# Interleaving the later stages of an image pipeline with its matrix-root stage on one TensorE

## The chip, the cores and the metric

The kernel runs on one core of one Trainium2 chip. The metric is the device time of one execution in microseconds (us). The kernel before takes 3546 us, with runs within 0.1% of each other.

## The reference, cut to what matters

`x` is 32 images of 32 channels of 128x128, float32. Two layers follow each other:

```python
def _L0_conv_ref(A):             # per channel matrix: square root by 5 Newton-Schulz steps
    Y = A2 / normA; Z = I
    for _ in range(5):
        T = 0.5 * (3.0 * I - Z @ Y)
        Y = Y @ T
        Z = T @ Z
    return Y * sqrt(normA)

def _L1_conv_ref(x, w1, w2):     # spectral layer: keep 64 x 32 modes, mix channels, go back
    x_dht = fftn(x).real
    top = einsum('bixy,ioxy->boxy', x_dht[:, :, :32, :32], w1)
    bot = einsum('bixy,ioxy->boxy', x_dht[:, :, -32:, :32], w2)
    ...
    return ifftn(out_dht).real

x = x + _L0_conv_ref(group_norm(x))
x = x + _L1_conv_ref(group_norm(x), weights1, weights2)
```

In the kernel the first layer is a chain of 128x128 matrix products for each of 1024 channel matrices ("root steps"). The second is, per image, a forward transform, then for all images together the products with the weights ("mode products"), then per image an inverse transform that is added to the layer's input.

## The kernel before

There are three stages, one after the other. The root stage runs four lanes, each a set of four channels, with the forward transforms woven in. Each image stays in one 2 MB tile and goes to DRAM (`mid`) with one store.

```python
while todo or any(lanes) or back:
    for i in range(LANES):
        ...                               # start a set, or take one step of lane i (newton)
    rounds += 1
    if back and next(back[0], back) is back:      # one step of statistics or forward transform
        back.pop(0)
```

Then come the mode products over 16 groups kk of modes. The weights come in three buffers, and the spectra of four kk at a time in 2 MB:

```python
for kk in range(KK):
    wt = wts[kk % 3]
    for l4 in range(4):
        nc.sync.dma_start(out=wt[rows, l4], in_=wk[kk, rows])
    if kk % 4 == 0:
        nc.scalar.dma_start(out=xk, in_=xs[:, :, kk : kk + 4, :]...)
    for h in range(2):
        ...                               # 16 matmuls into one PSUM bank, then a copy to om
    for q in range(4):
        nc.sync.dma_start(out=od[:, :, KK * q + kk], in_=om[32 * q : 32 * q + 32]...)
```

Then the inverses, where loads stand on one DMA queue (sync) and stores on another (scalar):

```python
for b in range(B):
    nc.sync.dma_start(out=ob, in_=od[b]...)
    nc.sync.dma_start(out=xt, in_=mid[b])
    for d in range(2):
        ...     # 32 matmuls of 64x32 into two banks (pg), per e: copy to gt, 2 matmuls of 512 (py)
                nc.vector.tensor_add(xt[:, o : o + 4, :], py[i], xt[:, o : o + 4, :])
    for i in range(2):
        nc.scalar.dma_start(out=out[b, :, 16 * i : 16 * i + 16, :], in_=xt[...])
```

Of the kernel before, what the change touches and what calls it, by code (L numbers as in the profile page):

```python
# [31 lines left out]
LANES = 4  # L33

# [18 lines left out]
def conv_preact_kernel(  # L53
# [35 lines left out]
    xs = dram.tile([B, P, KK, 32], F32, name="xs")  # L89
    od = dram.tile([B, 2, K, 16, L], F32, name="od")  # L90

    with ExitStack() as phase:
        xp = phase.enter_context(tc.tile_pool(name="xp", bufs=3))
        up = phase.enter_context(tc.tile_pool(name="up", bufs=1))
        nsp = phase.enter_context(tc.tile_pool(name="nsp", bufs=5))
        sp = phase.enter_context(tc.tile_pool(name="sp", bufs=2))
        small = phase.enter_context(tc.tile_pool(name="small", bufs=2))
        ps_ns = phase.enter_context(tc.tile_pool(name="ps_ns", bufs=5, space=PSUM))
        ps_ax = phase.enter_context(tc.tile_pool(name="ps_ax", bufs=2, space=PSUM))
        ps_st = phase.enter_context(tc.tile_pool(name="ps_st", bufs=1, space=PSUM))  # L100

        def root(v, n, tag, f=1.0):

            s0 = small.tile([P, n], F32, tag=f"{tag}_s0", name=f"{tag}_s0")
            nc.scalar.activation(s0, v, AF.Sqrt, scale=1.0 / (f * f))
            q = small.tile([P, n], F32, tag=f"{tag}_q", name=f"{tag}_q")
            nc.vector.reciprocal(q, s0)
            nc.vector.tensor_mul(q, q, v)
            nc.vector.scalar_tensor_tensor(q, q, 1.0 / (f * f), s0, ALU.mult, ALU.add)
            s = small.tile([P, n], F32, tag=f"{tag}_s", name=f"{tag}_s")  # L110
            nc.vector.tensor_scalar_mul(s, q, 0.5 * f)
            return s

        def moments(st, tag):



            f = st.rearrange("p (g c) (e t) -> p g (c e) t", c=2, t=3)
            ms = small.tile([P, G], F32, tag=f"{tag}_ms", name=f"{tag}_ms")
            nc.vector.tensor_reduce(ms, f[:, :, :, 1], AX.X, ALU.add)  # L120
            pm = ps_st.tile([P, 64], F32, tag="st", name=f"{tag}_pm")
            nc.tensor.matmul(pm[:, 0:G], avg_mean, ms, start=True, stop=True)
            nm = small.tile([P, G], F32, tag=f"{tag}_nm", name=f"{tag}_nm")
            nc.vector.tensor_copy(nm, pm[:, 0:G])  # L124
            d = small.tile([P, G, 4], F32, tag=f"{tag}_d", name=f"{tag}_d")
            nc.vector.tensor_tensor(
                d, f[:, :, :, 1], nm[:, :, None].to_broadcast([P, G, 4]), ALU.add
            )
            nc.vector.tensor_mul(d, d, d)
            nc.vector.scalar_tensor_tensor(  # L130
                d, d, 64.0, f[:, :, :, 2], ALU.mult, ALU.add
            )
            return ms, nm, d

        def prep(b, made):

            xt = xp.tile([P, C, P], F32, tag="xt", name=f"xt{b}")
            for i in range(4):
                nc.sync.dma_start(
                    out=xt[:, 8 * i : 8 * i + 8, :],  # L140
                    in_=xt_in[b, :, 8 * i : 8 * i + 8, :],
                )
            yield
            st = small.tile([P, C, 6], F32, tag="a_st", name=f"a_st{b}")
            for c in range(C):
                nc.vector.bn_stats(st[:, c, :], xt[:, c, :])
                if c % 8 == 7:
                    yield
            _, nm, d = moments(st, "a")
            q = small.tile([P, C], F32, tag="a_qs", name=f"a_qs{b}")  # L150
            nc.vector.tensor_reduce(
                q, d.rearrange("p g (c e) -> p (g c) e", e=2), AX.X, ALU.add
            )
            pq = ps_st.tile([P, 64], F32, tag="st", name=f"a_pq{b}")
            nc.tensor.matmul(pq[:, 0:C], avg_q, q, start=True, stop=True)
            yield

            v = small.tile([P, C + G], F32, tag="a_v", name=f"a_v{b}")
            nc.vector.tensor_copy(v[:, 0:C], pq[:, 0:C])
            vg = small.tile([P, G], F32, tag="a_vg", name=f"a_vg{b}")  # L160
            nc.vector.tensor_reduce(
                vg, v[:, 0:C].rearrange("p (g c) -> p g c", c=2), AX.X, ALU.add
            )
            nc.vector.tensor_scalar(v[:, C:], vg, 0.5, EPS, ALU.mult, ALU.add)
            s = root(v, C + G, "a_r")
            inv = small.tile([P, C + G], F32, tag="a_inv", name=f"a_inv{b}")
            nc.vector.reciprocal(inv, s)
            yield

            sc = small.tile([P, C], F32, tag="a_sc", name=f"a_sc{b}")  # L170
            nc.vector.tensor_scalar_mul(sc, inv[:, 0:C], 1.0 / P)
            n = small.tile([P, G, 2], F32, tag="a_n", name=f"a_n{b}")
            nc.vector.tensor_tensor(
                n,
                s[:, 0:C].rearrange("p (g c) -> p g c", c=2),
                inv[:, C:, None].to_broadcast([P, G, 2]),
                ALU.mult,
            )
            nn = small.tile([P, C], F32, tag="a_nn", name=f"a_nn{b}")
            nc.vector.tensor_scalar_mul(nn, n.rearrange("p g c -> p (g c)"), float(P))  # L180
            sn = root(nn, C, "a_t")

            scr = small.tile([P, C], F32, tag="a_scr", name=f"a_scr{b}")
            nc.vector.tensor_scalar_mul(scr, sc, QR)
            off = small.tile([P, G, 2], F32, tag="a_off", name=f"a_off{b}")
            nc.vector.tensor_tensor(
                off,
                scr.rearrange("p (g c) -> p g c", c=2),
                nm[:, :, None].to_broadcast([P, G, 2]),
                ALU.mult,  # L190
            )
            made[b] = (xt, nm, sc, sn, scr, off.rearrange("p g c -> p (g c)"))
            yield

        def bank(pool, tag):
            return pool.tile([P, 4, P], F32, tag=tag, name=tag)

        def taken(ps, tag, bufs=5, f=1.0):
            t = nsp.tile([P, 4, P], F32, tag=tag, name=tag, bufs=bufs)
            if f == 1.0:  # L200
                nc.scalar.copy(t, ps)  # L201
            else:
                nc.scalar.mul(t, ps, f)  # L203
            return t

        def plus(ps, f, t, tag, bufs=5):

            s = nsp.tile([P, 4, P], F32, tag=tag, name=tag, bufs=bufs)
            nc.vector.scalar_tensor_tensor(s, ps, f, t, ALU.mult, ALU.add)  # L209
            return s  # L210

        def products(lhsT, rhs):
            ps = bank(ps_ns, "ns")
            for j in range(4):
                nc.tensor.matmul(  # L215
                    ps[:, j, :], lhsT[:, j, :], rhs[:, j, :], start=True, stop=True
                )
            return ps

        def transposed(t):  # L220
            ps = bank(ps_ns, "ns")
            for j in range(4):
                nc.tensor.transpose(ps[:, j, :], t[:, j, :], ident)  # L223
            return ps

        raw = {}

        def fetch(b, g):
            t = nsp.tile([P, 4, P], F32, tag="b", name=f"b{b}_{g}", bufs=7)
            nc.sync.dma_start(  # L230
                out=t, in_=x[b, 4 * g : 4 * g + 4].rearrange("c h w -> h c w")
            )
            raw[b, g] = t

        def quartic(m, mb, r):


            v = plus(products(mb, m), -1 / (QA * QR), m, "v", 4)
            yield
            w = plus(transposed(v), -QA, r, "w", 4)  # L240
            yield
            q = plus(products(v, w), -QA / 16, eyes["eye_q"], "q")
            yield
            return q

        def newton(b, g, xt, nm, sc, sn, scr, off):


            chans = range(4 * g, 4 * g + 4)
            m = nsp.tile([P, 4, P], F32, tag="x", name="x0", bufs=6)  # L250
            mb = raw.pop((b, g))
            for j, c in enumerate(chans):
                nc.gpsimd.tensor_scalar(  # L253
                    m[:, j, :],
                    xt[:, c, :],
                    nm[:, c // 2 : c // 2 + 1],
                    sc[:, c : c + 1],
                    ALU.add,
# [32 lines left out]
            yield  # L291

        def post(b, xt):

            nc.sync.dma_start(out=mid[b], in_=xt)


# [263 lines left out]
```

## Time and profile before

| stretch of the profiled run | us | TensorE busy us | granted clock | DMA share |
|---|---|---|---|---|
| root stage | 0 to 3043 | 2997 | 1.00 | 0.20 |
| last spectrum and mode products | 3043 to about 3190 | a third | 0.69 in the middle | 0.75 |
| inverses | about 3190 to 3543 | two thirds | 0.83 | 0.96 |

The table reads: TensorE is full for 86% of the time while the DMA engines are a fifth busy, and then the DMA engines are full or nearly so and TensorE is not. "Granted clock" is the TensorE clock that the profile shows as allowed, as a share of full speed. "PE" is TensorE executing matmuls and "PEld" its weight loads. "DVE", "ACT" and "POOL" are VectorE, ScalarE and GpSimd. "SPq" is the in-order queue from which the sync engine issues transfers. A line such as "A <- B" says that A sat idle until B was done.

### The profile page before, as it was taken

The numbers are of one execution on the slowest core, as the hardware profiler recorded it, in microseconds if no ns is written. First come the engines' busy times: TensorE is split into PE (matmuls) and PEld (weight loads), VectorE is DVE, ScalarE is ACT, GpSimd is POOL, SyncE is SP. The second block draws the span as 40 slices with busy tenths as digits, with TensorE's granted clock in tenths as the row PEclk, the third lists the DMA queues.
The fourth block names the chain that finished last, engine by engine and source line by source line (L and its number), as shares of the span: only waits on it lengthen the run. The fifth ranks groups of instructions, "written<-read, shape, count | busy, mean of one in ns | idle before, by whom it ended". The sixth has DMA issues, their size and how long they took to land.

```text
span 3543.4 us, 77025 instructions
## 1 busy us (share of the span) xinstructions
PE 3297.4 (93%) x30912; PEld 2962.0 (84%) x30912; DVE 2302.1 (65%) x6401; ACT 1422.0 (40%) x2993; POOL 1092.1 (31%) x1544
## 2 busy tenths in 40 slices
PE   6999999999999999999999999999999999536776
PEld 6999999999999999999999999999999999433433
DVE  6666777776677677776667777776777765203544
ACT  4444444444444444444444444444444443101211
POOL 4333333333333333333333333333333332100000
PEclk9999999999999999999999999999999999777888
DMA  3221122221222222222221122211222210569999
GB/s 114 72 75 68 57 72 75 75 72 52 73 75 73 75 73 72 72 75 72 75 72 55 69 75 75 73 58 67 75 72 75 72 52 31 144 163 403 418 416 386
DMA packets 206390, 382.74 MB, mean 108 GB/s; under 512 B 11345, under 2 KB 158801, under 8 KB 189649
## 3 DMA queue, kind: packets, MB, share of 16 engines
q1 hardware_dynamic: 180368, 302.33, 24.2%
q10 hardware_dynamic: 25664, 75.50, 5.5%
q8 instruction: 243, 3.98, 0.5%
q14 instruction: 115, 0.93, 0.1%
HBM read 226.79 MB, written 150.99 MB: 107 GB/s over the span
## 4 chain that ended last, share of the span: by engine, by line
PE 83%; DMA 9%; DVE 3%; issue 2%; ACT 1%; SPq 1%; POOL 1%; ACTq 0%; DVEq 0%; POOLq 0%
PE ns L215 62%; PE ns L223 9%; PE ax L302 5%; DMA out<-yt 3%; DMA yt<-mid 2%; PE py L503 2%; DMA b<-in_x 2%; PE f L327 2%; PE ax L314 2%; DMA xk<-xs 1%; ACT spec L370 1%; PE pm L443 1%; POOL x L253 1%; DVE xt L288 1%; SPq L457 1%
## 5 line engine op out<-in xcount | busy, mean ns | idle before, releaser
L278 POOL TENSOR_TENSOR r<-mb,eye_d 128x512 f32<-128x512 f32 x256 | 325.3, 1271 | 1397.7 <-ACT mb L203 1190.3
L253 POOL TENSOR_SCALAR x<-xt,a_nm,a_sc 128x128 f32<-128x128 f32 x1024 | 445.2, 449 | 542.8 <-PE ns L215 522.6
L215 PE MATMUL ns<-w,v 128*128 128x128 f32 x4096 | 545.6, 276 | 7.2 <-DVE w L209 6.4
L215 PE MATMUL ns<-y,q 128*128 128x128 f32 x4096 | 542.2, 275 | 0.0
L215 PEld LDWEIGHTS ns<-w,v 128*128 128x128 f32 x4096 | 498.7, 192 | 36.8 <-DVE w L209 35.2
L261 ACT ACTIVATE b<-b,a_off,a_scr 128x128 f32<-128x128 f32 x1024 | 446.6, 485 | 192.4 <-DMA b<-in_x 156.9
L201 ACT COPY y<-ns 128x512 f32<-128x512 f32 x512 | 299.0, 584 | 513.4 <-PE ns L215 511.9
L215 PEld LDWEIGHTS ns<-y,q 128*128 128x128 f32 x4096 | 499.1, 192 | 0.0
L209 DVE SCALAR_TENSOR_TENSOR w<-ns,r 128x512 f32<-128x512 f32 x512 | 350.9, 685 | 75.6 <-PE ns L223 44.5
L209 DVE SCALAR_TENSOR_TENSOR q<-ns,eye_q 128x512 f32<-128x512 f32 x512 | 348.2, 680 | 36.2 <-PE ns L215 21.4
L209 DVE SCALAR_TENSOR_TENSOR v<-ns,m 128x512 f32<-128x512 f32 x256 | 176.1, 688 | 301.0 <-PE ns L215 301.0
L288 DVE SCALAR_TENSOR_TENSOR xt<-ns,a_t_s,xt 128x128 f32<-128x128 f32 x1024 | 287.3, 339 | 79.6 <-PE ns L215 79.1
L269 POOL TENSOR_TENSOR r<-b,eye_d 128x512 f32<-128x512 f32 x256 | 325.2, 1270 | 0.0
L223 PE MATMUL ns<-ident,v 128*128 128x128 f32 x2048 | 309.5, 274 | 1.0 <-DVE v L209 1.0
L209 DVE SCALAR_TENSOR_TENSOR v<-ns,x 128x512 f32<-128x512 f32 x256 | 176.4, 689 | 197.4 <-PE ns L215 196.9
L201 ACT COPY m<-ns 128x512 f32<-128x512 f32 x256 | 147.8, 577 | 376.9 <-PE ns L215 376.9
L215 PE MATMUL ns<-m,q 128*128 128x128 f32 x2048 | 279.5, 279 | 15.0 <-DVE q L209 15.0
L215 PEld LDWEIGHTS ns<-m,q 128*128 128x128 f32 x2048 | 248.7, 192 | 48.3 <-DVE a_nm L124 23.5
L508 DVE TENSOR_TENSOR yt<-py,yt 128x512 f32<-128x512 f32 x256 | 158.9, 684 | 189.7 <-PE py L503 175.0
L215 PE MATMUL ns<-x,b 128*128 128x128 f32 x2048 | 272.5, 276 | 5.1 <-POOL x L253 5.1
L215 PE MATMUL ns<-x,q 128*128 128x128 f32 x2048 | 274.7, 277 | 0.5 <-DVE q L209 0.5
L215 PE MATMUL ns<-q,t 128*128 128x128 f32 x2048 | 273.7, 277 | 0.0
(104 smaller groups left out, 4967.7 us busy)
## 6 DMA issues: line engine op xcount, KB each, us to landing
xt<-in_xt SPq DMA_DIRECT2D x128, 512.0 KB, 5.9
b<-in_x SPq DMA_DIRECT2D x256, 256.0 KB, 2.8
mid<-xt SPq DMA_DIRECT2D x32, 2048.0 KB, 6.3
yt<-mid SPq DMA_DIRECT2D x32, 2048.0 KB, 12.7
out<-yt ACTq DMA_DIRECT2D x64, 1024.0 KB, 17.6
xs<-spec SPq DMA_DIRECT2D x32, 256.0 KB, 2.0
xk<-xs ACTq DMA_DIRECT2D x4, 2048.0 KB, 13.4
wt<-in_wk SPq DMA_DIRECT2D x64, 128.0 KB, 2.9
```

Source lines behind the costliest of these rows:

```text
L201: nc.scalar.copy(t, ps)
L209: nc.vector.scalar_tensor_tensor(s, ps, f, t, ALU.mult, ALU.add)
L215: nc.tensor.matmul(ps[:, j, :], lhsT[:, j, :], rhs[:, j, :], start=True, stop=True)
L223: nc.tensor.transpose(ps[:, j, :], t[:, j, :], ident)
L253: nc.gpsimd.tensor_scalar(m[:, j, :], xt[:, c, :], nm[:, c // 2 : c // 2 + 1], sc[:, c : c + 1], ALU.add, ALU.mult,)
L261: nc.scalar.activation(mb[:, j, :], mb[:, j, :], AF.Identity, bias=off[:, c : c + 1], scale=scr[:, c : c + 1],)
L269: nc.gpsimd.tensor_tensor(r, mb, eyes["eye_d"], ALU.add)
L278: nc.gpsimd.tensor_tensor(r, mb, eyes["eye_d"], ALU.add)
L288: nc.vector.scalar_tensor_tensor(xt[:, c, :], ps[:, j, :], sn[:, c : c + 1], xt[:, c, :], ALU.mult, ALU.add)
L302: nc.tensor.matmul(ps[64 * i : 64 * i + 64], tab[:, T_FW], xt[:, 8 * q + 4 * i : 8 * q + 4 * i + 4, :], start=True, stop=True,)
L314: nc.tensor.transpose(ps[:, j, :], sw[:, j, :], ident)
L508: nc.vector.tensor_add(xt[:, o : o + 4, :], py[i], xt[:, o : o + 4, :])
```

## The change

The intent is to let the mostly idle DMA engines of the root stage do the work of the later stages. Images form two groups, 26 and 6. When the 26th image's spectrum is done, the first group's mode products and then its inverses are stepped between root steps of the last images. To make room in SBUF (the on-chip memory), images are held by sets of four channels: four-channel tiles instead of 2 MB tiles, half-size weight buffers (two instead of three), three PSUM banks (the memory that matmuls write to) for everything that is not a root step. The core of the diff, cut:

```diff
+GROUPS = (26, 6)
-    xs = dram.tile([B, P, KK, 32], F32, name="xs")
+    xs = [dram.tile([KK, P, n, 32], F32, ...) for i, n in enumerate(GROUPS)]
 ...
-            nc.sync.dma_start(out=mid[b], in_=xt)
+        for i, xt in enumerate(pair):
+            nc.sync.dma_start(out=mid[b][:, 8 * q + 4 * i : 8 * q + 4 * i + 4, :], in_=xt)
 ...
+    def fetch(b, g):
+        xt, t = four("xt", 10), four("b", 5)
+        nc.sync.dma_start(out=xt, in_=xt_in[b, :, 4 * g : 4 * g + 4, :])
+        nc.sync.dma_start(out=t, in_=x[b, 4 * g : 4 * g + 4].rearrange("c h w -> h c w"))
 ...
+    def load_input(b, d):                    # input of half an inverse: four tiles
+                nc.sync.dma_start(out=y, in_=mid[b][:, o : o + 4, :])
 ...
-                nc.scalar.dma_start(
-                    out=out[b, :, 16 * i : 16 * i + 16, :], in_=xt[:, 16 * i : 16 * i + 16, :]
-                )
+                for o, y in yts[b, d][2 * e : 2 * e + 2]:
+                    nc.sync.dma_start(out=out[b, :, o : o + 4, :], in_=y)
 ...
+            for queue in ((backs,), (preps,), (backs, specs), (posts,))[i]:
+                step(queue)                  # backs: mode products, then inverses, of a group
```

Every transfer of the changed kernel is issued from the one sync queue.

## The prediction

> **What bounds the kernel now.** I read the page's strips first, then the busy time by stretch. The strips (40 slices of 88.6 us) show two regimes:
>
> ```profile
> PE   6999999999999999999999999999999999536776
> ...
> DVE  6666777776677677776667777776777765203544
> ...
> PEclk9999999999999999999999999999999999777888
> DMA  3221122221222222222221122211222210569999
> ```
>
> For 34 slices TensorE is full and the DMA engines are a fifth busy; for the last six the DMA engines are full, TensorE is not, and its granted clock has fallen. Cut at the places where the lines change (columns: busy us and count of PE, PEld, DVE, ACT, POOL, then clock, DMA share, GB/s):
>
> ```profile
> 0.00:3043.00 3043.00, 2996.66 (x25256) 2785.02 (x25258) 2126.07 (x6114) 1342.17 (x2842) 1085.15 (x1542) 1.00 0.20 70
> 3043.00:3060.00 17.00, 4.76 (x26) 2.05 (x22) 6.03 (x15) 3.56 (x8) 6.96 (x2) 0.74 0.64 186
> 3060.00:3166.00 106.00, 33.80 (x768) 31.90 (x768) 8.30 (x12) 7.06 (x12) 0.00 (x0) 0.69 0.75 192
> 3166.00:3543.40 377.40, 262.19 (x4864) 143.00 (x4864) 161.68 (x260) 69.17 (x132) 0.00 (x0) 0.83 0.96 389
> ```
>
> The root stage ends at 3043 us with TensorE busy 98.5% at clock 1.00 (in windows of 500 us from 500 on, 99.3%; the rest is the start). Then comes a tail of 500 us: 17 us of last spectrum, mode products to about 3190, inverses to 3543, the latter at 389 GB/s with DMA 0.96 busy. The inverse moves 32 images at 352 us / 32 = 11 us each, set by the DMA engines; the chain of waits names the input load waiting for output stores (238 us on the queue of the load). So the aim of the change is right: put DMA-bound work beside a stage whose DMA engines are idle. But TensorE, the bound of that stage, must then do the moved work too.
>
> What it costs TensorE is read where TensorE ran it unhindered. One half image of the inverse, at granted clock 1.00:
>
> ```profile
> 3201.56 1.46 PE L486 MATMUL pg<-tab,ob 64*32 64x128 f32 x64
> ...
> 3203.16 1.99 PE L503 MATMUL py<-gt,tab 64*128 64x512 f32 x8
> ...
> 3205.07 1.82 PE L486 MATMUL pg<-tab,ob 64*32 64x128 f32 x110
> ```
>
> ...and two mode steps (at granted clock 0.66), with the store that follows:
>
> ```profile
> 3085.12 5.42 PE L443 MATMUL pm<-wt,xk 128*32 128x128 f32 x128 [7.14 <-DMA wt<-in_wk]
> ...
> 3089.59 6.19 SPq L457 DMA_DIRECT2D od<-om  x8
> ```
>
> From 3201.56 to 3205.07 is 3.5 us for half an image, 7.0 us for one. 128 mode instructions in 5.42 us at 0.66 are 28 ns each at full clock; a whole set of mode products is 512 matmuls, 1024 instructions, so 29 us.
>
> **What the Trainium skill says.** "TensorE: Matmul & The Clock Gate", Part 1, says that an idle TensorE falls to half clock and warms after about 3.4 us of work. The trace agrees in direction: 1.00 in the root stage, 0.69 in the mode products. Moved work therefore also runs faster. "TensorEngine Tiling (Array Packing)", Key Properties, says that changing the tiling mode drains TensorE. The trace fits: in the root stage the 64-column matmuls (L302) stand behind 16.1 us of idle time in 96 places, 0.17 us each. "DMA: Bandwidth & Descriptors", Specifications, says that transfers under 512 B are below line rate. No run yet shows it for the new spectrum store, which goes from 2 KB pieces to 128 B pieces.
>
> **The change part by part.** The built order, not only the diff, was compared (it has no times). Root matrices: the same 10240 products and the same transposes on TensorE, by the same four lanes in the same rotation, with fewer buffers per tag (w 4 to 3, y 5 to 4, mb 4 to 2). Distance between producer and consumer stays two or three groups of four matmuls (2 to 3 us) against a DVE step of 0.69 us, so I expect no change over the first 26 images, 95 us each.
>
> Mode products of the first 26 images start in the order at about two thirds of TensorE's root work, and all 26 inverses lie in its last fifth, ahead of the last root matrices. Only 512 mode matmuls and 6 of 32 inverses come after. Mode products are done twice in all: a matmul of 26 or 6 images costs what one of 32 costs (the moving side is the weights).
>
> TensorE work added before the end of the root stage:
> - 26 inverses x 7.0 us = 182 us.
> - Mode switches not in those 7.0 us: each inverse has six pieces set apart between root matrices, so about six more switches x 0.16 us = 1 us, x 26 = 26 us.
> - Mode products 29 us + 64 switches x 0.16 us = 39 us.
> - Bubbles: where the order puts the second step of an inverse right behind its first (the first four inverses, at an image boundary) TensorE must wait for ScalarE's copy (0.53 us) and DVE's addition (0.62 us). Summing what the order leaves short of 1.0 to 1.5 us gives 13 us; I take 15.
>
> Sum 262 us if all are taken whole; the pieces overlap a little with the root matrices' own waits, so I take 250. Root end: 3041 + 250 = 3291 us.
>
> DVE takes 26 x 8 x 0.62 us = 129 us more over that stretch of some 520 us. With 71% before, it stays near 70%, because the root steps are spread. The DMA engines get 26 x 4.25 MB = 110 MB, with 30 MB of root traffic about 270 GB/s, below the 389 to 400 seen. Both stay off the path.
>
> The tail that is left:
> - Last spectrum: from the last root product to the issue of the spectrum store, 9.7 us as before (3041.2 to 3050.9); its landing 2.0 us before, with 128 B pieces I estimate 5; first xk 3 us. 18 us.
> - Mode products of six images: 32 half steps with two buffers. The queue's order for each kk is: one weight load, four od stores, three weight loads, four more, one xk. The odd half step waits for matmuls 1.7 us, ScalarE copy 0.6, four stores x 0.55, weight issues 0.8, landing 2.4 (median 2.9, least 2.2): 7.7 us. 16 kk x 7.7 = 123 us. If stores of six images issue in 0.35 us instead of 0.55, it is 6.9 us, 110 us. I take 113. The old stage took about 122 us, with 2 MB xk loads of 12 to 14 us each, which vanish; but halving the buffers gives that back. Six images cost what 32 did.
> - Store and load between the stages: 2.4 + 2.7 = 5 us.
> - Six inverses, now with three PSUM banks instead of eight: per half image 2 us of L486, one copy 0.7, L503 1.5, addition 0.7, L503 1 = 5.9 us at a clock near 0.7; 12 us per image, 70 us. DMA no longer sets this, since 18 inputs are loaded ahead.
> - Last store and end: 8 us as before.
>
> Sum 214 us. Total: 3291 + 214 = 3505 us of span, and the median lies 2.8 us above the span: **3508 us**, 1.1% less than 3546. Balance: the tail shrinks from 502 to 214 (288 won), TensorE's root stretch grows by 250.
>
> **The rivals.**
> 1. *The tail goes away, with TensorE work nearly free.* Then the gain would be 250 us or more, 3300 us. For it: the inverse was DMA bound. Against it: TensorE has 0.7% of slack in the root stage, and 250 us of work cannot go into 20 us of slack.
> 2. *A smaller price on both sides:* pieces packed at 6.5 us per inverse, the six-image modes at 6 us per kk, the last inverses at 10 us each: 202 us added and a tail of 180 us, 3431 us, 3.3% faster. For it: a burst of 128 L486 ran in 2.06 us. Against it: pieces that short never stand alone in the new order.
> 3. *The root stage stalls.* All DMA issue moves onto one in-order queue: 1503 rows in the order against 460 before, and a store that waits for an addition holds back a fetch of the next matrices. Fewer buffers per tag also might cost 1% of 3041 us, 30 us. Then 3550 to 3600. Against it: 1503 x 0.35 us is 526 us of issue in 3300, and fetches run two sets (24 us) ahead.
>
> **Range and chances.** The root end is uncertain by 25 us (price of an inverse 6.5 to 8 us, bubbles 5 to 50), the tail by 25 (modes 95 to 125, inverses 58 to 78). Together 36 us, so 8 in 10 lies in about 3455 to 3565. The bound for 2% faster is 3475 us, about one such deviation below the middle: 0.17. Slower by 2% is above 3617 us, possible only through rival 3: 0.04. Within 2%: 0.79.
>
> **What would show each step.** The root's last product (the DVE line that writes xt) ends near 3291 us, with TensorE over 97% busy in the stretch of the inverses; if it is lower, rival 3. In the first 2000 us the images still come at 95 us. L506 and L489 in the root stretch together take about 7 to 8 us of PE busy per image. The last mode products take 105 to 123 us, about 7 us per kk, and DMA share there is far below 0.75. The last inverses come at about 12 us per image, with waits on the addition and the copy, not on DMA. The prediction fails if the root rate of the first 26 images changes, if fetches are late, or if the tail's mode products find another pace.

## The result, and the profile after

The changed kernel takes 3629 us (3625 to 3634, 4 runs), the kernel before 3546.5 us in the same rounds. The ratio is 1.0234 (95% interval 1.0216 to 1.0251): 2.3% slower, outside the predicted range. A ratio here is the mean time of one kernel's fast runs over the mean of the other's of the same rounds, so not quite the ratio of the medians. All timed runs were in the fast state. Where a run was one look without timed rounds, its state is unknown, and I read its trace by stretches. The 500 to 2500 us of root steps, which are the same in all of them, have equal TensorE busy time within 0.15% (1980 to 1983 us of 2000), except in the one run that the text names.

The strips of the page of the changed kernel, 40 slices of 90.6 us:

```profile
PE   6999999999999999999999999999989898999546
...
PEclk9999999999999999999999999999999899999658
DMA  6332332332233333333233333333457766776537
```

The DMA engines are now busy while the root still runs (slices 29 to 37 of 40), as intended. But TensorE shows eights in the same slices, and the last three slices, the new tail, are as empty as the old one. By stretch (columns as in the prediction: busy us and count of PE, PEld, DVE, ACT, POOL, then clock, DMA share, GB/s) these are the mode products of the 26 images among root steps, their inverses among root steps, the last spectrum with the six images' mode products, and their inverses:

```profile
2529.90:2759.70 229.80, 213.37 (x2479) 195.74 (x2478) 110.45 (x303) 89.63 (x177) 60.07 (x83) 0.96 0.50 140
2759.70:3373.70 614.00, 555.24 (x6571) 412.69 (x6570) 347.61 (x797) 203.67 (x414) 111.56 (x155) 0.95 0.71 229
3373.70:3533.30 159.60, 68.00 (x1048) 51.09 (x1048) 4.10 (x22) 21.33 (x37) 0.00 (x0) 0.58 0.35 94
3533.30:3611.80 78.50, 55.42 (x864) 26.85 (x856) 28.53 (x44) 12.40 (x23) 0.00 (x0) 0.79 0.68 227
```

The root ends at 3374 us instead of the predicted 3291. In the inverses' stretch TensorE is idle 59 us of 614, and its clock is 0.95. The tail from there is 252 us instead of 214.

What TensorE waited for is seen in one gap of that stretch (timeline: start, duration, engine, line, operation, count; in brackets the idle time before and its releaser):

```profile
2942.73 3.69 SPq L468 DMA_DIRECT2D yt<-mid  x3
...
2946.53 1.58 SPq L249 DMA_DIRECT2D b<-in_x  x1
...
2951.27 1.26 ACT L266 ACTIVATE b<-b,a_off,a_scr 128x128 f32<-128x128 f32 x3 [7.66 <-DMA b<-in_x]
2952.44 1.04 ACT L499 COPY gt<-ps 128x512 f32<-128x512 f32 x2
2953.05 0.50 PEld L506 LDWEIGHTS ps<-gt,tab 64*128 64x128 f32 x4 [5.47 <-ACT gt L499]
2953.05 2.08 PE L506 MATMUL ps<-gt,tab 64*128 64x512 f32 x4 [5.23 <-ACT gt L499]
...
2958.42 1.13 PE L506 MATMUL ps<-gt,tab 64*128 64x512 f32 x4
```

Read it downwards. The sync queue spends 3.7 us on three loads for an inverse. Only then it issues the fetch of a root matrix (`b`). ScalarE waits 7.7 us for that fetch, and the copy that an inverse needs stands behind it in ScalarE's own order. TensorE waits 5.2 us for the copy. The four matmuls after the gap take 2.08 us, the same four 1.13 us a little later: the gap also lowered the clock. The Trainium skill's "TensorE: Matmul & The Clock Gate", Part 1, says that an idle TensorE falls to half clock, and this trace agrees. The gap is not all queue: from its issue to ScalarE's step the fetch takes 4.7 us. Pairing every fetch of `b` with ScalarE's first step on it in the trace, the median of this time is 4.7 us in the stretch and 3.2 us in root steps alone (1000 to 2000 us).

The largest waits in the inverses' stretch, of the queue and of ScalarE for a fetch:

```profile
SPq L468 <- DMA out<-yt: 215.4, 141, 5.3
SPq L520 <- DVE yt L511: 82.7, 72, 8.9
...
ACT b L266 <- DMA b<-in_x: 121.4, 21, 11.8
```

Loads of an inverse (L468) wait 215 us for the store that frees their buffer to land; stores (L520) wait 83 us for the addition. All waits of that queue are 374 us, and the issue of its 531 transfers takes 237 us in the trace: together 611 of 614 us. That sum alone says little, because a queue that always has a next transfer either waits or issues. In no_inv_dma, the run without these transfers (below), it is 491 + 48 of 547 us. What differs is whose waits they are. In no_inv_dma 167 us are fetches of root matrices that wait for their own buffers (L248 and L249), so they go out as early as they can. Here it is 12 us: when a fetch comes up, its buffer is mostly free already, and what held it is what stood before it.

In the tail, one step kk of the six images' mode products:

```profile
3408.59 1.94 PE L427 MATMUL ps<-wt,xk 128*32 128x128 f32 x32 [3.02 <-DMA wt<-in_wk]
...
3411.20 3.02 SPq L440 DMA_DIRECT2D od<-om  x4
3412.56 0.59 ACT L436 COPY om<-ps 128x512 f32<-128x512 f32 x1 [1.39 <-PE ps L427]
3414.26 3.23 SPq L410 DMA_DIRECT2D wt<-in_wk  x7
3417.28 1.51 PEld L427 LDWEIGHTS ps<-wt,xk 128*32 128x32 f32 x32 [5.07 <-issue]
3417.31 1.94 PE L427 MATMUL ps<-wt,xk 128*32 128x128 f32 x32 [4.85 <-DMA wt<-in_wk]
```

8.7 us from matmuls to matmuls, of which 3.0 us are the issue of four stores that the next weights stand behind.

### The profile page after: what moved, and what is told of

It is laid out like the page before. It is cut to its first block, busy times and chain, and to the rows that moved or that the text cites. A ratio compares the mean times of both kernels' runs of the same rounds, so it can differ in the third digit from the quotient of the medians.

```text
span 3625.5 us, 81572 instructions
## 1 busy us (share of the span) xinstructions
PE 3366.5 (93%) x31936; PEld 3002.7 (83%) x31936; DVE 2268.6 (63%) x6384; ACT 1464.8 (40%) x3041; POOL 1093.8 (30%) x1546
## 3 DMA queue, kind: packets, MB, share of 16 engines
q14 instruction: 132, 1.08, 0.1%
## 4 chain that ended last, share of the span: by engine, by line
PE 60%; issue 12%; DVE 11%; DMA 9%; POOL 5%; SPq 2%; ACT 2%; POOLq 0%; ACTq 0%; DVEq 0%
PE ps L235 42%; PE ps L241 7%; PE ps L506 4%; DMA b<-in_x 3%; DMA xs<-in_xt 3%; POOL x L258 3%; PE ps L318 2%; POOL r L274 2%; DVE a_st L166 2%; PE ps L427 2%; PE ps L489 2%; SPq L440 1%; DMA out<-yt 1%; DVE q L229 1%; DVE w L229 1%
## 5 line engine op out<-in xcount | busy, mean ns | idle before, releaser
L235 PE MATMUL ps<-w,v 128*128 128x128 f32 x4096 | 553.1, 278 | 5.3 <-DVE w L229 5.3
L235 PE MATMUL ps<-y,q 128*128 128x128 f32 x4096 | 543.8, 276 | 0.0
L235 PEld LDWEIGHTS ps<-w,v 128*128 128x128 f32 x4096 | 504.6, 194 | 20.8 <-issue 12.9
L235 PEld LDWEIGHTS ps<-y,q 128*128 128x128 f32 x4096 | 499.0, 192 | 6.6 <-issue 6.6
L229 DVE SCALAR_TENSOR_TENSOR w<-ps,r 128x512 f32<-128x512 f32 x512 | 350.8, 686 | 138.8 <-PE ps L241 131.1
L221 ACT COPY y<-ps 128x512 f32<-128x512 f32 x512 | 299.7, 585 | 299.9 <-PE ps L235 299.8
L229 DVE SCALAR_TENSOR_TENSOR q<-ps,eye_q 128x512 f32<-128x512 f32 x512 | 347.9, 679 | 43.0 <-PE ps L235 29.6
L309 DVE SCALAR_TENSOR_TENSOR xt<-ps,a_t_s,xt 128x128 f32<-128x128 f32 x1024 | 292.5, 341 | 48.1 <-PE ps L235 46.4
L241 PE MATMUL ps<-ident,v 128*128 128x128 f32 x2048 | 316.7, 275 | 2.0 <-DVE v L229 2.0
L235 PE MATMUL ps<-x,q 128*128 128x128 f32 x2048 | 282.1, 281 | 1.4 <-DVE q L229 1.4
```

The lines of the kernel that those rows point to most:

```text
L221: nc.scalar.copy(t, ps)
L229: nc.vector.scalar_tensor_tensor(s, ps, f, t, ALU.mult, ALU.add)
L235: nc.tensor.matmul(ps[:, j, :], lhsT[:, j, :], rhs[:, j, :], start=True, stop=True)
L241: nc.tensor.transpose(ps[:, j, :], t[:, j, :], ident)
L309: nc.vector.scalar_tensor_tensor(xt[:, j, :], ps[:, j, :], sn[:, c : c + 1], xt[:, j, :], ALU.mult, ALU.add)
```

## The experiments

**Theory A**: all transfers share one queue that issues in order. In the inverses' stretch its own waits hold back the fetches of the root matrices, ScalarE and GpSimd wait for those, and TensorE idles and slows. **Rival B**: the DMA engines have not the throughput for these packets of 2 KB, whatever the queue. **Rival C**: TensorE's own chain through three PSUM banks and the copies. **Rival D**: the pieces are bunched badly in TensorE's order. "Root end" is the start of the last step that writes `xt` (the DVE line of the sum), 3374 us in the changed kernel.

| run | root end us | TensorE idle in the inverses' stretch us | last root step to last mode matmul us | median us | ratio to before (95%) |
|---|---|---|---|---|---|
| changed kernel | 3374 | 59 | 160 | 3629 | 1.0234 (1.0216 to 1.0251) |
| no_inv_dma (wrong on purpose) | 3311 | 12 | 153 | 3556 (one look) | |
| inv_late | 3107 | not among root steps | | 3693 (one look) | |
| out_act | 3364 | 51 | 153 | 3616 | 1.0204 (1.0187 to 1.0221) |
| fetch_pool | 3513 | | | 3746 | 1.0578 (1.0556 to 1.0601) |
| ahead | 3372 | 60 | 157 | 3622 | 1.0220 (1.0205 to 1.0236) |
| yt10 | 3367 | 53 | 162 | 3613 (one look) | |
| fetch_act | 3343 | 45 | 157 | 3598 | 1.0151 (1.0134 to 1.0168) |
| od_act | 3352 | 52 | 118 | 3560 (one look) | |
| od_fetch_act | 3329 | 41 | 120 | 3538 | 0.9980 (0.9971 to 0.9989) |
| od_act_out_pool | 3340 | 45 | 117 | 3547 (one look) | |
| half_bytes (wrong on purpose) | 3335 | 23 | 154 | 3580 (one look) | |
| three_queues | 3307 | 27 | 114 | 3510 | 0.9907 (0.9891 to 0.9922) |

### no_inv_dma: the inverses without their transfers

The result is wrong on purpose: images 0 to 25 are not written. TensorE's order is that of the changed kernel but for a few neighbouring rows.

```diff
-                nc.sync.dma_start(out=y, in_=mid[b][:, o : o + 4, :])
+                if where[b][0]:
+                    nc.sync.dma_start(out=y, in_=mid[b][:, o : o + 4, :])
-                    nc.vector.tensor_add(y, py[i], y)
+                    nc.vector.tensor_add(y, py[i], y if where[b][0] else eyes['eye15'])
-                    nc.sync.dma_start(out=out[b, :, o : o + 4, :], in_=y)
+                    if where[b][0]:
+                        nc.sync.dma_start(out=out[b, :, o : o + 4, :], in_=y)
```

> Wrong on purpose: the inverses of the first 26 images neither load their input (a constant is added) nor store their result; the order on TensorE is the changed kernel's, unchanged. Theory A (the one in-order DMA queue makes the fetches of the next matrices late, ScalarE and GpSimd wait for them, TensorE idles and its clock falls): the last root product moves from 3374 us to about 3300 us, idle TensorE in the stretch of the inverses falls below 20 us and the clock there is 1.00. Rival C (TensorE's own chain with three PSUM banks and the copies): the root still ends near 3370 us. Rival D (the placing of the pieces in the order, bunched at an image boundary): no more than 15 us of gain.

The root ends at 3311 us, 63 us earlier. The same stretch in this run:

```profile
2764.10:3311.00 546.90, 535.33 (x6571) 400.44 (x6570) 346.45 (x798) 204.41 (x414) 111.20 (x155) 1.00 0.22 66
```

It has the same 6571 matmul records as the changed kernel. The stretch is 67 us shorter: 47 us less idle (11.6 instead of 58.8), and 20 us less busy time for the same records, with the clock at 1.00 instead of 0.95. TensorE's work, banks, copies and order are unchanged, so rivals C and D have at most the 12 us of idle time that is left. A and B both remain.

### inv_late: the inverses after the root stage

```diff
-                backs.append(inverse(b))
+                late.append(inverse(b)) if i == 0 else backs.append(inverse(b))
 ...                                         # late is put ahead of backs when all lanes are empty
```

> The mode products of the first 26 images stay between the root steps, but all 26 inverses wait for the end of the root stage. All theories: the root ends near 3041 + 7 (later start) + 39 (mode products) + some waits = 3090 to 3105 us. It prices the mode products: if it ends later than 3115 us, the mode products cost more than I took. Total: 3100 + 26 inverses at 12 us or more + a tail of 250 us = 3660 to 3720 us.

The root ends at 3107 us and the total is 3693 us: inside the total's range, 2 us above the root end's. This run prices the parts. Before, the last such step began at 3041. This run is 5 us behind the kernel before by 2500 us (16792 root matmul records instead of 16824 by that time, at 0.15 us each; an estimate), all from the start. So the 26 images' mode products cost 3107 - 3041 - 5 = 61 us. From here to no_inv_dma it is 3311 - 3107 = 204 us for 26 inverses on TensorE, 7.8 us each. The transfers add the last 63 us.

### out_act and fetch_pool: one kind of transfer on another queue

```diff
-                    nc.sync.dma_start(out=out[b, :, o : o + 4, :], in_=y)          # out_act
+                    nc.scalar.dma_start(out=out[b, :, o : o + 4, :], in_=y)
```

> Only the stores of the result go back to ScalarE's queue, as in the kernel before. Theory A: the queue of the fetches is no longer held by stores that wait for an addition (83 us), but loads of the inverses that wait for a buffer (215 us) still stand in it, and ScalarE now waits for the additions in order; so a partial gain or a loss, total 3580 to 3650 us. Rival B: no change, 3629 us.

It gained 10 us of root end and 13 us in all: the partial gain. Against the kernel before its verdict at 2% is unclear. The gain came with the loads' wait grown from 215 to 370 us on the sync queue.

```diff
-        nc.sync.dma_start(out=xt, in_=xt_in[b, :, 4 * g : 4 * g + 4, :])            # fetch_pool
+        nc.gpsimd.dma_start(out=xt, in_=xt_in[b, :, 4 * g : 4 * g + 4, :])
 ...                                         # likewise the fetch of b and of the statistics
```

> The fetches of the root matrices and of the statistics go on GpSimd's DMA queue, all else stays. Theory A: fetches no longer stand behind stores and loads of the inverses; the root ends near 3300 us, the total near 3555 us. Rival B (the DMA engines themselves are slow with 2 KB pieces, whatever the queue): fetches stay late, the root ends at 3350 us or later, total about 3610 us or more. A cost of GpSimd's own issue may show in the first 2500 us.

This was a miss: by its numbers it fell on B's side, and only its cause speaks for A. The loss is not in the inverses' stretch. By 2500 us it has issued 15960 root matmul records instead of 16795, 5% fewer. In a stretch of root steps alone (1000 to 2000 us) the waits are:

```profile
POOL r L298 <- ACT mb L223: 364.5, 74, 8.7
...
ACT b L266 <- DMA b<-in_x: 183.8, 81, 5.3
```

GpSimd has a step that waits for ScalarE, and a fetch placed behind it is issued late. ScalarE waited 87 us for that fetch in the changed kernel over the same 1000 us, 184 us here. It is the theory's mechanism on another engine, in a place where it hurts for the whole run. Each issue also takes GpSimd 0.54 to 0.78 us (medians by kind), which no other run separates from the waiting.

### ahead and yt10: more lead, more buffers, same queue

```diff
-        xt, t = four("xt", 10), four("b", 5)                                        # ahead
+        xt, t = four("xt", 11), four("b", 6)
+    fetch(*fetches.pop(0))                   # one more fetch before the first set is staged
```

> Each fetch of a root matrix is issued one set (12 to 16 us) earlier, with one more buffer for each of its two tiles and one spectrum buffer fewer; queue, packets and bytes stay. Theory A (the fetch arrives late because it stands behind loads and stores of the inverses in one in-order queue): a set of lead is more than the waits seen (least 4, most 12 us), so ScalarE's waits for the fetch in the stretch of the inverses fall from 130 us to below 40, and the root ends at 3310 to 3325 us instead of 3374; total near 3570 us. Rival B (the DMA engines have not the throughput for these packets): the waits move to other tiles and the root ends above 3355 us.

```diff
-    spare = [("yt", 8)]                                                             # yt10
+    spare = [("yt", 10)]
```

> Ten input buffers for the inverses instead of eight (one spectrum buffer fewer). The loads' wait for the landing of a store (215 us on the queue) should fall by a half; theory A then has the root end 20 to 40 us earlier (3335 to 3355 us). If the bound is the throughput of the DMA engines, no change (3374 us).

Both expectations missed, and by the numbers both came out on B's side. In ahead the root still ends at 3372 us, and ScalarE still waits 112 us for `b` in the stretch. But the trace shows that this edit did not test what it was meant to. A fetch of `b` is issued 70 us before its first matmul instead of 58 (medians, 1000 to 2000 us), one set more as intended; from its issue to ScalarE's step on it there are still only 3.3 us instead of 3.2. ScalarE's step moved forward with the fetch, and it is ScalarE that waits. With ten buffers (yt10) the loads still wait 212 us for stores (215 before): more buffers did not take the wait away. A likely reason, not shown, is that the order places a load as soon as it reckons its buffer free, so that it again stands directly behind the store that it waits for. A and B both remained.

### fetch_act, od_act, and both: other kinds on ScalarE's queue

```diff
-        nc.sync.dma_start(out=xt, ...)  # and b, and the statistics                  # fetch_act
+        nc.scalar.dma_start(out=xt, ...)
```

> All fetches (root matrices and statistics) go on ScalarE's queue, so they never stand behind the inverses' transfers; ScalarE then waits in order for their buffers. Theory A: the root ends at 3300 to 3330 us, total near 3560 us, if ScalarE's own waits do not cost more. Rival B: no gain, the root ends above 3355 us.

```diff
-                    nc.sync.dma_start(                                              # od_act
+                    nc.scalar.dma_start(
                         out=od[i][:, :, KK * q + kk],
```

> Only the stores of the mode products go on ScalarE's queue. My estimate of the last mode products took a store to be issued in 0.55 us; it took 0.76, four per step, ahead of the next weights. Off that queue, the step of two halves should fall from 8.8 us to about 6.5 us, the last mode products from 141 us to about 105 us, and the first 26 images' mode products should leave less idle time on TensorE (16 us there). Total about 3590 us. If the step is instead set by the landing of the weights, it stays above 8 us.

> The stores of the mode products and the fetches go on ScalarE's queue; the other queue keeps the inverses' loads and stores. The two gains alone were 22 and 30 us of root end, 24 us of the last mode products for the first. Theory A: they add up, root end near 3320 us, last mode products 118 us, total near 3535 us. If they share one cause, root end stays near 3340 and the total near 3550.

fetch_act ends the root at 3343 us, 30 us earlier but 13 above its range (the total is 38 above the 3560 foreseen), so the fetches are only a part of what the queue holds back. The loads and additions of the inverses are still late, and TensorE meets them in its own order too. od_act ends it at 3352, and its total of 3560 is 30 below the one foreseen. Where the mode stores are off the queue, the 26 images' mode products leave TensorE idle 3 us instead of 16 (this run's stretch):

```profile
2532.10:2721.10 189.00, 186.06 (x2268) 167.00 (x2270) 103.86 (x298) 82.20 (x170) 53.63 (x77) 1.00 0.64 186
```

The six images' mode products run from 3371.4 to 3469.7 us: 98 us, or 6.1 us per kk, instead of 137 us and 8.6. (The "24 us" in the last expectation compares two different stretches; measured alike, the gain is 39 to 42 us.) Both together (od_fetch_act) end the root at 3329 us, 45 us earlier, so the gains nearly add (22 + 30 = 52), and the total is 3538 us, where about 3535 was foreseen.

### half_bytes: the same transfers with half the bytes

```diff
+                nn = 4 if where[b][0] else 2
-                nc.sync.dma_start(out=y, in_=mid[b][:, o : o + 4, :])
+                nc.sync.dma_start(out=y[:, 0:nn, :], in_=mid[b][:, o : o + nn, :])
 ...                                         # likewise the store; the addition as in no_inv_dma
```

> Wrong on purpose: the inverses of the first 26 images load and store only two of the four channels of each set (a constant is added in place of the input), so the same count of transfers is issued in the same order with half the bytes. If the throughput of the DMA engines is the cause of the 63 us that the inverses' transfers cost (rival B), the root ends 30 us or more earlier than 3374 us (below 3345). If issue and waits on one queue are the cause (theory A), at most 15 us earlier, as far as shorter landings shorten the waits.

The root ends at 3335 us, 39 us earlier, so by the expectation as written it speaks for B. The waits of the queue say how bytes come in. With half of them a store lands sooner, and the loads' wait for it falls from 215 to 118 us. Bytes therefore matter, but the run alone does not tell whether because the engines are at their limit or because the queue stands still while they land.

### od_act_out_pool and three_queues: nothing behind the loads

```diff
-                    nc.sync.dma_start(out=out[b, :, o : o + 4, :], in_=y)
+                    nc.gpsimd.dma_start(out=out[b, :, o : o + 4, :], in_=y)
 ...                                         # od stores on nc.scalar; in three_queues the fetches too
```

> Stores of the mode products on ScalarE's queue, stores of the result on GpSimd's. Fetches still stand behind loads of the inverses that wait for a store to land. Theory A in its narrow form (those waits, 215 us, are what delays the fetches): root end as in the run with the mode stores alone, 3352 us. If it is the sum of issue and waits that fills the queue: root end near 3325 us. GpSimd's own issue may cost it some us in its steps.

> All of it: fetches and mode stores on ScalarE's queue, result stores on GpSimd's, the inverses' loads alone with the input stores on the third. Theory A: root end 3300 to 3315 us, like the run without the inverses' transfers (3311), total 3515 to 3530 us, below the kernel before. Rival B: root end 3335 us or later, no better than fetches and mode stores moved.

With stores of the result on GpSimd's queue and mode stores on ScalarE's, the root ends at 3340 us, between the two values foreseen. With the fetches moved as well it ends at 3307 us, inside its range, and the total is 3510 us, 5 below its range. The same stretch, the same queue and ScalarE's wait in three_queues:

```profile
2712.30:3306.70 594.40, 567.56 (x6789) 430.65 (x6789) 365.55 (x843) 212.45 (x433) 233.04 (x375) 0.98 0.74 241
```
```profile
SPq L468 <- DMA out<-yt: 439.9, 184, 9.9
...
ACT b L266 <- DMA b<-in_x: 101.6, 25, 6.9
```

All the bytes are moved, at 241 GB/s instead of 229, and the DMA share is slightly higher. So the engines' throughput was not what cost most of the 63 us. The wait of loads for stores has even doubled, to 440 us, and costs little, because no fetch of a root matrix, no mode store and no result store stands behind it any more. That separates the two: the wait itself is nearly harmless, and its place ahead of other work in one order is not.

The root end of 3307 must not be read against the 3311 of no_inv_dma, where the mode stores were still on the sync queue. Against od_act (3352), which has them moved too, three_queues gains 45 us. Set against the 63 us, some 18 are left (an estimate, which takes the 22 us of od_act to lie outside the 63): TensorE is idle 27 us in the stretch instead of 12, at a clock of 0.98 instead of 1.00. ScalarE still waits 102 us for `b` (121 in the changed kernel, 52 in no_inv_dma), though at most 6.9 us at once instead of 11.8, and from issue to ScalarE's step a fetch takes 5.0 us (median; 4.7 in the changed kernel, 3.3 in half_bytes, 3.0 in no_inv_dma). So these fetches do land later beside the inverses' bytes, on the one queue and on three, and B may hold that part; no run settles it. Nor do the runs separate the order of issue from the order in which the engines serve the transfers of one queue, since a transfer that moves changes both.

This version is 0.9% faster than the kernel before (ratio 0.9907; by the verdict at 2%, the same) and 3.3% faster than the changed kernel (medians of different rounds).

## Why the prediction was wrong

It foresaw 3505 us of span and got 3625.5. By its own steps:

| step | predicted us | measured us | shown by |
|---|---|---|---|
| later start | 0 | 5 | root matmul records by 2500 us |
| 26 images' mode products among root steps | 39 | 61 | inv_late |
| 26 inverses on TensorE, switches and bubbles (after its rounding to 250) | 211 | 204 | no_inv_dma less inv_late |
| transfers of the inverses beside root steps | 0 | 63 | changed kernel less no_inv_dma |
| **root end later by** | **250** | **333** | |
| last spectrum to the first mode matmul | 18 | 23 | trace |
| six images' mode products | 113 | 137 | trace, od_act |
| store and load between | 5 | 8 | trace |
| six inverses | 70 | 74 | trace |
| last store and end | 8 | 10 | trace |
| **tail** | **214** | **252** | |

- **Right: what TensorE pays.** The sum for 26 inverses was 211 us against 204, and the root rate of the first 26 images did not move. TensorE was the engine that had to pay, so rival 1 (work nearly free) was wrong, as argued.
- **Failed: "Both stay off the path."** The step set the DMA work against the engines' bandwidth and found room. The bandwidth was there for most of it, as three_queues shows (241 GB/s and the root end 67 us earlier). What was missing is the path by which the transfers are issued: in one in-order queue the fetches stood behind the inverses' waits, ScalarE stood behind the fetches, and TensorE behind ScalarE, which with the slower clock cost most of the 63 us.
- **Failed: the reasons against rival 3.** The rival itself was the right one: "a store that waits for an addition holds back a fetch of the next matrices". It was dismissed with "1503 x 0.35 us is 526 us of issue in 3300". That is a mean over the whole run, while the transfers lie in a sixth of it. It also counted issue time only. In that sixth, the waits that stand in the queue (374 us, of which 341 are the inverses' own loads and stores) are larger than the issue time (237 us). The second reason, "fetches run two sets (24 us) ahead", looked at the wrong engine. In root steps alone a fetch of `b` is issued 58 us before its first matmul, but 3.2 us before ScalarE's step on it, and ScalarE waits there 64 times in 1000 us (87 us in all). There was no lead where it was needed. The result even lies above the 3550 to 3600 us that the rival was given.
- **Mis-sized: the mode step.** The mechanism was written down correctly (four stores issued ahead of the next weights), but the store was first taken at the 0.55 us of the old kernel and then lightened toward 0.35 us because it has fewer pieces. It took 0.76 us in the tail. With 3.0 us of stores in place of 2.2, the 7.7 us of the sum become 8.5, against 8.6 measured. The same stores delayed the 26 images' mode products by some 13 us of TensorE's time (idle 16 us, 3 us in od_act), which is most of the 22 us missing in that line.
- **Overlooked: the clock.** The prediction quotes that moved work runs faster at full clock, but not that waits inside the root stage take the clock from the root's own matmuls: 20 of the 63 us.
- **Slips on which nothing rests.** Rival 2's parts give 3041 + 202 + 180 + 3 = 3426 us and not 3431. By the root's end the trace of the changed kernel has 1592 transfers issued and not 1503 (447 in the kernel before).

What stays open: the 18 us that three_queues does not win back; why the issue of a mode store takes 0.76 to 0.81 us where the old one took 0.59; and how the 63 us divide between fetches and the inverses' own late loads and stores, since moved one kind at a time they gave 10 to 30 us each, and ScalarE's wait for fetches fell only from 121 to 102 us in three_queues while TensorE's idle time more than halved.

## What to carry to other kernels

When a stage's transfers are moved beside another stage, treat the issuing queue as an engine of its own that works in order: ask of each fetch which issues and which waits of other transfers stand before it, in the stretch where they will lie and not over the whole run. A queue's waits and issues can fill its time and do no harm (539 of 547 us in no_inv_dma), so look at whose waits they are. Transfers that wait for a landing or for a computation belong in a different queue from fetches that another stage needs on time; where that is so, the waits may be long and cost little. And measure the lead of a fetch up to the first engine that waits for it in order (here ScalarE, 3 us), not up to the engine that needs the result in the end (TensorE, 58 us).

## What the Trainium skill lacked or had wrong

- "DMA: Bandwidth & Descriptors", section "Issuing engines are not separate DMA queues", says that issuing from several engines at once only saves the sequencer's time to initiate a transfer, usually small beside the transfer. The section leaves out that a transfer also waits, on its queue, for what the transfers before it wait for. Here the same transfers spread over three queues ended the root stage 67 us earlier (3374 to 3307) and cut the total from 3629 to 3510 us. In the one queue, 374 us of waits stood beside 237 us of issue in a stretch of 614 us.
- The same page's "Issuing engine by pattern" calls GpSimd's queue generally more flexible and the other two generally faster. The runs add where it fits: stores on it won (three_queues against od_fetch_act: 3538 to 3510 us), at 0.54 us of GpSimd each, and fetches on it lost (3629 to 3746 us), where GpSimd's own steps that wait for ScalarE held the fetches back (ScalarE's wait for them rose from 87 to 184 us in 1000) and each issue took 0.54 to 0.78 us of GpSimd.
- No page gives, for this chip, the time that one issue takes on its queue by kind of transfer; the same page only counts cycles of an issue for unnamed "previous generations". Here the medians on the sync queue were 0.33 to 0.42 us for a plain 256 KB load or store and 0.81 us for the mode stores of 104 KB or less (0.70 to 1.08).
